# A four-layer transformer kernel on one core: table writes, recurrence steps and the order around two layer boundaries rearranged

## The chip, the core and the metric

The kernel runs on one core of a Trainium2 chip. The metric is the device time of one launch in microseconds. Each run is one execution; the figure shown is the median of three.

## What is computed

The reference takes 2048 tokens of 512 channels (8 sequences of 256) and sends them through four layers. Each layer has an attention-like part and a feed-forward part, both gated by a tanh and added to the tokens:

```python
x = x + tanh(g_xattn[0]) * L0_xattn(layernorm(x), ctx, ...)   # quantised attention
x = x + tanh(g_ffn[0])   * L0_ffn(layernorm(x), ...)          # one of 8 low-rank experts
x = x + tanh(g_xattn[1]) * L1_xattn(layernorm(x), ctx, ...)   # linear attention
x = x + tanh(g_ffn[1])   * L1_ffn(layernorm(x), ...)          # 8 of 64 experts, and a shared one
x = x + tanh(g_xattn[2]) * L2_xattn(layernorm(x), ctx)        # channels attend to channels
x = x + tanh(g_ffn[2])   * L2_ffn(layernorm(x), ...)          # dense, 2048 hidden units, GELU
x = x + tanh(g_xattn[3]) * L3_xattn(..., layernorm(x), ctx)   # a recurrence over 256 steps
x = x + tanh(g_ffn[3])   * L3_ffn(layernorm(x), ...)          # 2 of 8 experts, and a shared one
```

## The kernel before

**Tiles and blocks.** The tokens stay in SBUF as 16 tiles `xt[0..15]` of 128 tokens by 512 channels. Most loops run over 4 blocks of 512 tokens (`NB`, each `TB` = 4 tiles), and many over the 2 sequences of a block (`bb`). Matrix products go to PSUM banks of pools `mm` (4 banks), `ac` (2) and `tr` (2, for transposes).

**What sets the order.** The program is written as generators that interleave pieces of several stages, and a scheduler then orders the instructions of each engine: among those whose inputs it believes ready it takes the one that comes first in the program. Each engine then works strictly in its order, so an instruction that waits holds up all behind it. `behind(one, other, ...)` (line 131) forces `one` to stand after `other` in that order without a semaphore. `latest[0]` is the last matmul of the latest product.

**Layer 1.** `attend1` (833) does the attention of a block and calls `step`, which advances a generator of routing pieces and then, through `write` (945), issues rows of the routing table. A row write is an indirect DMA on POOL of 128 rows; it waits for the end of the product `latest[0]`. `route1(q)` (969) handles a pair of tiles q: norm, logits, the choice of 8 experts, the rows and weights (`hit`, line 1064), and it appends 16 writes to `pending`. The last pair, q = 7, writes its rows at once and also ranks the experts. `shared1(blk)` (1087) is the shared expert of a block in 5 pieces: gate, up, the remainder (which ends with the units `hT`, line 1110), and two down products of two tiles each, whose results are added by `add_scaled` (219) on DVE. After block 3's attention, the pieces of blocks 0 to 2 are interleaved with pair 7's routing and with `write(3, latest[0])` (1163). Then the table is read back (1177, `rows`, after all writes), turned by PE into `who_ps` (1193) and copied into `who` and `share`; each pair of experts gathers its tokens `xg` by `who` (1213). The experts' results are added in DRAM to two accumulators.

**The seam to layer 2.** After the experts comes `shared1` of block 3 (1336). `combine` (1344) loads the two accumulators (`more`) and adds them to the tokens on DVE. The first two tiles' combine is issued before the down products of block 3. Layer 2 then begins with `norm_of` for each sequence of block 0 (1729) and the scores.

**Layers 2 and 3 interleaved.** `xattn2` (1369) computes for each sequence of a block 4 score products (`s`), their maximum on DVE (1385), an exponential on ACT (1387, `E`), a scaling `vs` on DVE (1391), then 4 output products `o`. `ffn2` (1436) has 4 quarters of 4 hidden products `h2p` and 4 output products `o2f`. Meanwhile `step(n, one)` advances `tail(blk)`, which is layer 3 for the block before: the recurrence `xattn3` (1471), four channel groups with scans on DVE, products on POOL and an exponential on ACT, then turned by PE (`y`, 1543) and added; and the routing `route` (1621), which ends with 8 table writes on POOL (1669). `held` ties the first recurrence operation of a step behind `one`. At the last quarter's first output `last` flushes what is left with `step(1000)`. `ready2` (1416) norms a block for `ffn2` during the second half of `xattn2`. In block 3 the tail is interleaved with the shared expert `shared3`.

Of the kernel before, what the change touches and what calls it, by code (L numbers as in the profile page):

```python
# [20 lines left out]
P = 128  # L21
# [25 lines left out]
def flamingo_kernel(ctx: ExitStack, tc: tile.TileContext, a):  # L47
# [103 lines left out]
    def stats_of(ts_, name, after=()):  # L151
# [15 lines left out]
        yield ts_, mv, rstd  # L167

    def normed(stats, name, after=()):
        ts_, mv, rstd = stats  # L170
        out = []
        for i, t in enumerate(ts_):
            xn = xnp.tile([P, C], F32, tag="xn", name=f"xn_{name}_{i}")
            one = nc.vector.tensor_scalar(xn, xt[t], mv[:, i, 0:1], rstd[:, i : i + 1], ALU.subtract, ALU.mult)
            for other in after:
                behind(one, other, "the scores first")
            out.append(xn)
        return out

# [466 lines left out]
    def middle():  # L646
        with ExitStack() as st:
# [185 lines left out]
            def attend1(blk, one_step):  # L833
# [24 lines left out]
                for bb in range(BLK // S):  # L858
                    nm = f"{blk}_{bb}"
                    kf, V = context1(blk, bb, K, step) if bb else first  # L860
                    if blk == NB - 1 and bb:
                        step = lambda n: one_step(n, True)
# [65 lines left out]
                    for nt in range(2):  # L928
                        aoT = t2.tile([P, KC, P], F32, tag="t2", name=f"aoT_{nm}_{nt}")
                        aoTs.append(aoT)  # L930
                        transpose4(aoT, aos[nt].rearrange("p h d -> p (h d)"), f"ao_{nm}_{nt}")
                        step(1)
                    for nt in range(2):
                        ps = mmtile(f"wo1_{nm}_{nt}")
                        matmul_k(ps, [aoTs[nt][:, k, :] for k in range(KC)], [wo[:, k, :] for k in range(KC)])
                        i = blk * TB + bb * 2 + nt
                        add_scaled(i, ps, tg[:, 1:2])
                        step(2 if nt == 0 else 0)
                    done.append(blk * (BLK // S) + bb)
# [29 lines left out]
            def route1(q):  # L969
# [92 lines left out]
                for i in range(2):  # L1062
                    for j in range(K1):
                        nc.vector.scalar_tensor_tensor(
                            hit, key[:, i, :], key8[:, i, j : j + 1], w[:, i, :], ALU.is_equal, ALU.mult,
                            accum_out=pay[:, i, j, 1:2],
                        )
                    nc.vector.tensor_scalar(
                        pay[:, i, :, 1], pay[:, i, :, 1], den[:, i : i + 1], None, ALU.mult
# [9 lines left out]
                if q == 2 * NB - 1:  # L1079
                    ordered(expert)  # L1080
                    yield

            I1R = I1 - P
            rows_of = (slice(0, I1R), slice(FD, FD + I1R))
            rest1 = rows_of[1]

            def shared1(blk, shgu):

# [19 lines left out]
                for n in range(2):  # L1108
# [3 lines left out]
                    )  # L1112
                last_add[:] = [one]
                yield
                for i in range(0, TB, 2):
                    ps = [mmtile(f"shd{blk}_{i + n}") for n in range(2)]
                    last = None
                    for k in range(2):
                        for n in range(2):
                            rows = rows_of[n] if k else slice(0, P)  # L1120
                            one = nc.tensor.matmul(
                                ps[n], hT[k][rows, ts(i + n, P)], shd[rows, k, :], start=(k == 0), stop=(k == 1)
                            )
# [17 lines left out]

            last_add = []
            gen = work()
# [48 lines left out]
            for n in range(2):  # L1192
                one = nc.tensor.transpose(who_ps[:, n, :], rows[:, :, n], ident)
# [163 lines left out]

    kxvs, kx_load, first_loads = {}, [], []

# [9 lines left out]
    def xattn2(blk, xns, pools, step, ready=iter(())):  # L1369
# [4 lines left out]
        for bb in range(BLK // S):  # L1374
# [6 lines left out]
            for ec in range(KC):  # L1381
# [53 lines left out]

    def ffn2(blk, b8, wp, b1, gb2, step, last):
        xT = turned2.pop(blk)

        for q in range(HID // BLK):
            h = b8.tile([P, KC, BLK], F32, tag="b8", name=f"h2_{q}_{blk}")  # L1440
            p2 = []
            for j in range(KC):
# [109 lines left out]
    def back():  # L1552
        with ExitStack() as st:
# [63 lines left out]
            row_i = lp.tile([P, TT, 2], I32, tag="row3", name="row3")  # L1617
            writes = []
            xT = []

            def route(blk):
# [45 lines left out]
                for t in range(blk * TB, blk * TB + TB):  # L1667
                    for j in range(2):
                        one = nc.gpsimd.indirect_dma_start(
                            out=table[:, :],  # L1670
                            out_offset=bass.IndirectOffsetOnAxis(ap=row_i[:, t, j : j + 1], axis=0),
                            in_=pay[:, t, j, :],
                            in_offset=None,
                        )
                        tc.declare_no_dep(one.ins, group="table3", reason="choices have slots of their own")
                        tc.add_to_no_dep_group("table3", one.ins)
                        writes.append(one)
                    if t % 2:
                        yield

# [59 lines left out]
            for blk in range(NB):  # L1740
                ffn2(blk, fp, wp, b1, gb2, step, lambda i: last(blk + 2, i))
                rest.append(tail(blk))
# [83 lines left out]
            def shared3():  # L1826
# [5 lines left out]
                for blk in range(NB):  # L1832
                    xb = [xT[blk][:, k, :] for k in range(KC)]
                    hT = late.tile([P, 6, BLK], F32, tag="shT3", name=f"shT3_{blk}")
                    for m in (5, *range(5)):
# [13 lines left out]
                        else:  # L1849
# [248 lines left out]
```

## Time and profile before

| | us |
|---|---|
| median of 3 runs | 2705.74 (2701.91 to 2705.78) |
| the profiled execution | 2704.81 |
| its span, first to last instruction | 2703.0 |
| TensorE (PE) busy | 2553.9, 94% |
| VectorE (DVE) busy | 1288.3, 48% |
| GpSimd (POOL) busy | 890.6, 33% |
| ScalarE (ACT) busy | 671.9, 25% |
| mean granted TensorE clock | 0.974 |

Stages by time from the span's start: layer 0 to about 560, layer 1's attention to 911, shared expert and table to 984, layer 1's experts to 1491, the seam to 1518, layer 2 with the recurrence to 2145, layer 3's experts to the end.

In the profile, a group of instructions is named by its line, engine, operation and tiles. PEld is PE's weight load, SPq the queue of DMAs issued by SP. An idle time in brackets is the time that the engine stood before the instruction, and after the arrow what ended it. The granted clock is the share of full speed that TensorE was given.

### The profile page before, as it was taken

The page shows a single profiled execution, that of the slowest core. Times are in us where ns is not written, and L with a number is a line of the kernel's source. Part 1 is how long each engine was busy: PE and PEld are TensorE (multiplying, and loading weights), DVE is VectorE, ACT ScalarE, POOL GpSimd, SP SyncE. Part 2 cuts the span into 40 slices and gives each one's busy share as a digit, 9 for nine tenths or more (in the row PEclk, how much of TensorE's full clock was granted, in tenths as well). Part 3 has the DMA queues.
Part 4 walks back from the last instruction along what each step waited for, and adds up shares of the span by engine and source line. Part 5 has one row for each costly group of instructions (what it writes and reads, how often), then busy time and mean ns, then how long its engine had stood idle before and what let it go on. Part 6 is the DMA issues. An engine that isn't in the chain of part 4 may idle for free. (4 is left out here: it accounts for less than half of the span.)

```text
span 2703.0 us, 29475 instructions
## 1 busy us (share of the span) xinstructions
PE 2553.9 (94%) x10253; PEld 1355.1 (50%) x10268; DVE 1288.3 (48%) x3535; ACT 671.9 (25%) x1505; POOL 890.6 (33%) x814
## 2 busy tenths in 40 slices
PE   7889898999999899999999899898999999999998
PEld 3445444455665445555555344344454444455554
DVE  7656575536655622222222641767666674121121
ACT  2534344311111113333333211222223231111110
POOL 1111110112444445656565110333333342333332
PEclk9999899999999899999999999999999999999999
DMA  5000000112200259999997721132121211888884
GB/s 214 9 16 24 20 36 4 33 36 63 64 25 25 59 175 237 246 242 246 243 241 169 224 113 64 38 110 61 61 91 67 106 16 47 278 276 270 288 278 113
DMA packets 96187, 333.04 MB, mean 123 GB/s; under 512 B 20608, under 2 KB 23041, under 8 KB 88098
## 3 DMA queue, kind: packets, MB, share of 16 engines
q0 software_dynamic: 45856, 156.51, 23.0%
q1 hardware_dynamic: 47154, 170.34, 18.6%
q10 hardware_dynamic: 3024, 4.25, 0.5%
q8 instruction: 84, 1.38, 0.2%
q14 instruction: 69, 0.57, 0.1%
HBM read 280.46 MB, written 64.91 MB: 128 GB/s over the span
## 5 line engine op out<-in xcount | busy, mean ns | idle before, releaser
L210 PE MATMUL gu<-w,eb 128*128 128x352 f32 x896 | 285.9, 462 | 0.0
L1293 POOL DMA_INDIRECT acc<-eb,who x112 | 177.5, 1585 | 175.5 <-DVE eb L102 148.3
L210 PE MATMUL h2p<-xnT_f,p 128*128 128x512 f32 x512 | 228.0, 601 | 3.0 <-ACT xnT_f L104 3.0
L210 PE MATMUL o2f<-p,h 128*128 128x512 f32 x512 | 224.8, 593 | 0.0
L210 PEld LDWEIGHTS gu<-w,eb 128*128 128x128 f32 x896 | 162.6, 192 | 73.4 <-issue 2.3
L950 POOL DMA_INDIRECT table<-pay,rowi x128 | 126.1, 985 | 120.6 <-issue 26.1
L539 ACT ACTIVATE pr<-pr,n 128x256 f32<-128x256 f32 x256 | 127.9, 501 | 151.7 <-DVE n L534 148.8
L210 PEld LDWEIGHTS h2p<-xnT_f,p 128*128 128x128 f32 x512 | 97.2, 192 | 120.8 <-issue 115.7
L210 PEld LDWEIGHTS o2f<-p,h 128*128 128x128 f32 x512 | 96.2, 190 | 117.4 <-issue 115.2
L1213 POOL DMA_INDIRECT xg<-xnd,who x112 | 117.2, 1046 | 59.6 <-PE ehp L1240 22.8
L221 DVE SCALAR_TENSOR_TENSOR x<-o2f,tg,x 128x512 f32<-128x512 f32 x64 | 47.0, 739 | 140.7 <-PE o2f L210 140.7
L1768 PE MATMUL g_r<-w,xgT 128*128 128x352 f32 x288 | 111.7, 469 | 0.7 <-ACT xgT L104 0.7
L1768 PE MATMUL u_r<-w,xgT 128*128 128x352 f32 x288 | 108.7, 459 | 0.0
L1284 PE MATMUL ed<-w,eb 128*128 128x512 f32 x224 | 105.7, 594 | 0.9 <-DVE eb L1241 0.9
L102 DVE COPY eb<-ed 128x512 f32<-128x512 f32 x56 | 38.7, 692 | 138.6 <-PE ed L1284 138.6
L1775 DVE SCALAR_TENSOR_TENSOR h_r<-a_r,share,u_r 128x352 f32<-128x352 f32 x36 | 20.9, 581 | 175.9 <-PE u_r L1768 167.4
L1791 PE MATMUL d_r<-w,hT_r 128*128 128x512 f32 (+1 forms) x216 | 104.2, 592 | 0.0
L534 DVE CUSTOM_DVE_ANT_0 pr<-s,mask 128x256 f32<-128x256 f32 x256 | 96.9, 417 | 12.2 <-PE s L514 8.8
L1230 DVE SCALAR_TENSOR_TENSOR eb<-eb,share,gu 128x176 f32<-128x176 f32 x112 | 44.0, 393 | 122.0 <-ACT eb L1229 122.0
L591 POOL TENSOR_TENSOR y<-y,gbo 128x512 f32<-128x512 f32 x16 | 20.4, 1272 | 246.8 <-DVE y L590 239.0
L188 PEld LDWEIGHTS tr_xg<-ident,xg 128*128 128x128 f32 x592 | 68.9, 141 | 63.2 <-issue 49.9
L188 PE MATMUL tr_xg<-ident,xg 128*128 128x128 f32 x592 | 92.7, 280 | 6.4 <-DMA xg<-xnd,who 6.3
(534 smaller groups left out, 4730.5 us busy)
## 6 DMA issues: line engine op xcount, KB each, us to landing
w<-in_w SPq DMA_DIRECT2D x64, 960.0 KB, 7.3
p<-in_p SPq DMA_DIRECT2D x64, 512.0 KB, 5.7
xnd<-xn_f SPq DMA_DIRECT2D x32, 256.0 KB, 3.2
acc<-xnd SPq DMA_DIRECT2D x32, 256.0 KB, 4.9
more<-acc SPq DMA_DIRECT2D x32, 256.0 KB, 4.3
wd<-in_wd SPq DMA_DIRECT2D x64, 96.0 KB, 6.9
ctxTa<-in_ctxT SPq DMA_DIRECT2D x4, 1024.0 KB, 6.0
x<-in_x SPq DMA_DIRECT2D x16, 256.0 KB, 5.9
```

Source lines behind the costliest of these rows:

```text
L188: one = nc.tensor.transpose(ps[:, k, :], src[:, ts(k, P)], ident)
L210: one = nc.tensor.matmul(ps, lhsT[k], rhs[k], start=(k == 0), stop=(k == n - 1))
L221: return nc.vector.scalar_tensor_tensor(xt[i], ps, scale, xt[i], ALU.mult, ALU.add)
L534: one = nc.vector.tensor_tensor_reduce(pr[:, nt, :], ps[r][:, nt, :], mask[:, nt, :], -1.0, -LOW, ALU.add, ALU.min, n16[:, nt, h : h + 1],)
L539: nc.scalar.activation(pr[:, nt, :], pr[:, nt, :], AF.Exp, bias=n16[:, nt, h : h + 1], scale=-1.0, accum_out=s16[:, nt, h : h + 1],)
L950: one = nc.gpsimd.indirect_dma_start(out=table[:, :], out_offset=bass.IndirectOffsetOnAxis(ap=rows, axis=0), in_=choice, in_offset=None, b ...
L1213: nc.gpsimd.indirect_dma_start(out=xg, out_offset=None, in_=xnd[:, :], in_offset=bass.IndirectOffsetOnAxis(ap=who[:, c : c + 1], axis=0), ...
L1230: nc.vector.scalar_tensor_tensor(self.h, self.h, share[:, c : c + 1], gu[:, I1 : 2 * I1], ALU.mult, ALU.mult)
L1284: one = nc.tensor.matmul(ps[n], t.hT[rows, k, :], wd, start=(k == 0), stop=(k == 1))
L1293: nc.gpsimd.indirect_dma_start(out=acc[n][:, :], out_offset=bass.IndirectOffsetOnAxis(ap=who[:, t.c : t.c + 1], axis=0), in_=t.x, in_offse ...
L1768: nc.tensor.matmul(ps[:, 0:I3], xTt[:, k, :], wgu[k][:, g, :], start=(k == 0), stop=(k == KC - 1))
L1791: one = nc.tensor.matmul(ps, hT[:cn, n, :], wd[n][:cn], start=(n == 0), stop=(n == 2))
```

## The change

- `attend1`: in the second sequence of block 3 (`quiet`), the steps at the turned outputs and at the output product issue no table writes; they still advance the routing.
- `route1`: pair 7's first hit is ordered behind the shared expert's units made last (`hidden`).
- The table is read and turned before the two down products of block 2: only 13 of the 15 pieces of `shared1` run first, and the first of the remaining matmuls stands behind the turned order. `who` stands behind the units and no longer behind the adds.
- `shared1` of block 3 uses the `ac` banks for its first two tiles and leaves its four adds in a list; they are issued in layer 2 behind the last normed tile of the first two tiles (`latest_norm`).
- `combine` adds the tiles of blocks 2 and 3 on POOL instead of DVE.
- `xattn2`: no step during the second sequence's scores.
- `route`: the 8 table writes of a block go to a list. `ffn2` and, for block 2's, `shared3` issue one after each hidden (or gate and up) product of the next block, each waiting for that product's end. The last block's are issued at once.

```diff
-                    if blk == NB - 1 and bb:
+                    quiet = blk == NB - 1 and bb
+                    if quiet:
                         step = lambda n: one_step(n, True)
...
-                        step(1)
+                        step(0 if quiet else 1)
...
-                        step(2 if nt == 0 else 0)
+                        step(0 if nt or quiet else 2)
...
+                        if hidden and i + j == 0:
+                            behind(one, hidden[0], "the shared expert's first")
...
-            def shared1(blk, shgu):
+            def shared1(blk, shgu, later=None):
...
-                last_add[:] = [one]
+                hidden[:] = [one]
                 yield
                 for i in range(0, TB, 2):
-                    ps = [mmtile(f"shd{blk}_{i + n}") for n in range(2)]
+                    bank, tag = (mm, "mm") if i or later is None else (ac, "ac")
+                    ps = [bank.tile([P, BLK], F32, tag=tag, name=f"shd{blk}_{i + n}") for n in range(2)]
...
+                            if turned:
+                                behind(one, turned.pop(), "the table's order first")
...
-                        one = add_scaled(blk * TB + i + n, ps[n], tg[:, 5:6])
-                        if i + n == 0:
-                            behind(one, last_add[0], "its place")
-                        last_add[:] = [one]
+                        if later is None:
+                            add_scaled(blk * TB + i + n, ps[n], tg[:, 5:6])
+                        else:
+                            later.append((blk * TB + i + n, ps[n], tg[:, 5:6]))
...
-            while next(two, 0) is None:
+            for _ in range(5 * (NB - 1) - 2):
+                next(two)
                 write(3, latest[0])
                 with tc.high_priority(offset=400):
                     next(one, 0)
...
+            turned.append(one)
             who = l2.tile([P, P], I32, tag="who", name="who")
             one = nc.vector.tensor_copy(who, who_ps[:, 0, :])
-            behind(one, last_add[0], "the table comes late")
+            behind(one, hidden[0], "the table comes late")
             share = l2.tile([P, P], F32, tag="share", name="share")
             nc.scalar.copy(share, who_ps[:, 1, :])
+            for _ in two:
+                pass
...
-            end = shared1(NB - 1, again)
+            end = shared1(NB - 1, again, last_adds)
             for _ in range(3):
                 next(end)
-            first_loads.append(combine(range(2), adds=last_add))
+            first_loads.append(combine(range(2), adds=hidden))
...
-                add = nc.vector.tensor_tensor(xt[t], xt[t], more, ALU.add)
+                add = (nc.vector if t < 2 * TB else nc.gpsimd).tensor_tensor(out=xt[t], in0=xt[t], in1=more, op=ALU.add)
...
                 if bb:
                     latest_dve[:] = [one]
                     next(ready, None)
-                step(1, one)
+                else:
+                    step(1, one)
...
                 step(2 if q < 1 else 3, one)
+                write(1, latest[0])
...
+                    pending3.extend((row_i[:, t, j : j + 1], pay[:, t, j, :]) for j in range(2))
+                if blk == NB - 1:
+                    write3(len(pending3))
+                yield
+
+            def write3(n, after=None):
+                for _ in range(min(n, len(pending3))):
+                    rows, choice = pending3.pop(0)
+                    one = nc.gpsimd.indirect_dma_start(
...
+                    if after is not None:
+                        tc.add_manual_dep(
...
                 xns += norm_of(tiles, f"a2{bb}_")
+                other = latest_norm[0]
+                for add in last_adds:
+                    behind(add_scaled(*add), other, "layer 2's first tokens first")
+                last_adds.clear()
...
                         last_mul[:] = [one]
+                        write3(1, latest[0])
                         yield
```

More of the change, by code (lines that the diff above doesn't have):

```diff
@@ L167, in stats_of @@
         yield ts_, mv, rstd
+    latest_norm = []
     def normed(stats, name, after=()):
@@ L177, in normed @@
             out.append(xn)
+        latest_norm[:] = [one]
         return out
@@ L1063, in route1 @@
                     for j in range(K1):
-                        nc.vector.scalar_tensor_tensor(
+                        one = nc.vector.scalar_tensor_tensor(
                             hit, key[:, i, :], key8[:, i, j : j + 1], w[:, i, :], ALU.is_equal, ALU.mult,
@@ L1081, in route1 @@
                     yield
+            turned = []
+            hidden = []
             I1R = I1 - P
@@ L1140, in work @@
                     yield from route1(q)
-            last_add = []
             gen = work()
@@ L1356, in combine @@
         return one
-    kxvs, kx_load, first_loads = {}, [], []
+    kxvs, kx_load, first_loads, last_adds = {}, [], [], []
     def load_kx(b, b8, after=None):
@@ L1434, in ready2, with ffn2 @@
                 yield
-    def ffn2(blk, b8, wp, b1, gb2, step, last):
+    def ffn2(blk, b8, wp, b1, gb2, step, last, write):
         xT = turned2.pop(blk)
@@ L1617, in back @@
             row_i = lp.tile([P, TT, 2], I32, tag="row3", name="row3")
-            writes = []
+            writes, pending3 = [], []
             xT = []
@@ L1667, in route @@
                 for t in range(blk * TB, blk * TB + TB):
[L1668 to L1673, printed above, removed]
-                        )
[L1675 to L1679, printed above, removed]
+                    pending3.extend((row_i[:, t, j : j + 1], pay[:, t, j, :]) for j in range(2))
[6 more added lines that the diff above has]
+                    one = nc.gpsimd.indirect_dma_start(
+                        out=table[:, :],
+                        out_offset=bass.IndirectOffsetOnAxis(ap=rows, axis=0),
+                        in_=choice,
+                        in_offset=None,
+                    )
+                    if after is not None:
+                        tc.add_manual_dep(
+                            one.ins,
+                            after.ins.name,
+                            mybir.DependencyInfo(mybir.DependencyClass.Sync, mybir.DependencyReason.DATA),
+                            reason="one after the other",
+                        )
+                    tc.declare_no_dep(one.ins, group="table3", reason="choices have slots of their own")
+                    tc.add_to_no_dep_group("table3", one.ins)
+                    writes.append(one)
             def tail(blk):
@@ L1740, in back @@
             for blk in range(NB):
-                ffn2(blk, fp, wp, b1, gb2, step, lambda i: last(blk + 2, i))
+                ffn2(blk, fp, wp, b1, gb2, step, lambda i: last(blk + 2, i), write3)
                 rest.append(tail(blk))
```

## The prediction

> **What bounds the kernel now.** I read the page's busy table, then the waits of PE, then busy time and clock by stage, then the order of instructions around each long wait of PE.
>
> ```profile
> PE 2553.9 (94%) x10253; PEld 1355.1 (50%) x10268; DVE 1288.3 (48%) x3535; ACT 671.9 (25%) x1505; POOL 890.6 (33%) x814
> ```
>
> TensorE works 2553.9 of 2703.0 us. A time saved elsewhere counts only if PE waits for it; the chain of waits on the page names only the last store, so I go by PE's waits (what waits on what: total, times, longest).
>
> ```profile
> PE s L210 <- DMA kxvs<-in_ctx: 8.0, 2, 6.1
> PE tr_f L188 <- DVE xn_f L174: 8.0, 5, 5.3
> ...
> PE tr_xg L188 <- DMA xg<-xnd,who: 6.3, 1, 6.3
> PE o L210 <- ACT E L1387: 6.0, 2, 5.7
> ...
> PE shd L1121 <- DVE shT L1110: 3.4, 1, 3.4
> ```
>
> Five single waits of 3.4 to 6.1 us, and one of 5.25 us at 1517.71, lie where the diff works. Each costs more than itself. By stages (start:end, length, busy of PE, PEld, DVE, ACT, POOL, granted clock, DMA share, GB/s):
>
> ```profile
> 936.00:948.00 12.00, 11.91 (x19) 4.18 (x20) 5.63 (x24) 0.00 (x0) 7.26 (x8) 0.60 0.02 3
> ```
>
> A granted 0.60 over 12 us means 9.6 us at half speed, right after the 3.40 us wait at 936.09; the same follows the waits at 916.96, 983.86, 1517.71 and 1713.00. Half of such a stretch is lost work. Now the order of events (start, length, engine, what, idle before and its releaser):
>
> ```profile
> 914.49 0.97 POOL L950 DMA_INDIRECT table<-pay,rowi  x1 [0.30 <-issue]
> 915.48 0.75 POOL L166 TENSOR_TENSOR rstd_f<-ve_f,mhalf 128x2 f32<-128x2 f32 x1
> ...
> 916.96 1.94 PE L188 MATMUL tr_f<-ident,xn_f 128*128 128x128 f32 x8 [5.32 <-DVE xn_f L174]
> ...
> 964.76 1.02 POOL L1177 DMA_INDIRECT rows<-table,row_c  x1 [6.03 <-DMA table<-pay,rowi]
> ...
> 977.01 0.51 PE L1193 MATMUL who_ps<-ident,rows 128*128 128x128 f32 x2
> ```
>
> ```profile
> 1710.61 0.69 DVE L1511 TENSOR_TENSOR_SCAN aa<-ex,ev 128x256 f32<-128x256 f32 x1 [2.58 <-POOL ev L1508]
> 1711.22 0.67 DVE L1385 TENSOR_REDUCE m<-s 128x1 f32<-128x512 f32 x1
> ...
> 1713.00 12.56 PE L210 MATMUL o<-E,kxvs 128*128 128x512 f32 x24 [5.66 <-ACT E L1387]
> ```
>
> See in the first: the norm's power waits in POOL's queue behind table writes, PE behind it; and the table's rows were asked for at 964.76 but turned only at 977.01. In the second: a maximum of the second scores, which PE had ready near 1702, stands on DVE behind a recurrence scan.
>
> **Part 1, the quiet last block.** Eight writes (905.51 to 914.49, 1.275 us apart) leave POOL's queue there. The variances are ready at 911.0, so the power starts near 911.2 instead of 915.48 and PE goes on at 912.6: 4.3 us. The slow stretch 917 to 922 (transposes 1.94 against 1.04, shg 1.92 against 1.02, logits 2.54 against 1.89) goes: 2.45. The eight writes come back later on the same queue, see Part 3.
>
> **Part 2, the hits after the shared expert's units.** Units shT were made at 935.62, behind 8 hits and the ranking; their input was ready at 930.5. Put first, they leave PE about 0.6 of the 3.40: 2.8 us. From 936.09 to the next product at 947.94 PE took 11.85 us for ten down matmuls (10/16 of 5.84) and eight of 3.44 in all, 7.1 us: 4.75 more. The hits start 0.9 us later (two multiplications); nobody but the table's writes needs them. Parts 1 and 2: 14.3 us, so PE ends block 2's last shared product at 971.17 - 14.3 = 956.9.
>
> **Part 3, the table's order before the last two down products.** Now 32 writes (16 of tile pair 6, 16 of pair 7) follow one another on POOL from 914.8: 32 x 1.275 = 40.8, plus some 2 of waits for products, the last at 956 instead of 957.75. The weight loads that ran beside the old last writes (landing 5.9) start with `order`, now some 14 us sooner, so I take the usual 2.1 to land and 2.8 for the read (its row): rows at 961. PE waits there about 4.1 (new: before, the rows had 9.4 us to spare). Behind the order come 5.84 us of products, slowed by up to 2.9, beside the 6.34 us of copy, gather and landing that PE waited for bare. Gather transposes then start at 961 + 1.0 + 8.2 = 970.2 at full clock; before, 983.86 and 6.4 us at half speed, worth 987.1. **Saved 16.9 us** for Parts 1 to 3. Bounds: 23.3 if the rows are in time (956.9 + 0.5 + 6.34 = 963.7); 7.6 if writes and landing are late by 9 (979.5). I take 16.9, by the rows' usual landings. The experts' stage after it runs PE at 200.00 of 200.00 us, so it only shifts.
>
> **Part 4, the seam.** Four of block 3's adds (0.75 + 2.06 us on DVE) leave the way of the first norm: scores start at 1514.6 instead of 1517.71. But the second pair's norm has the same DVE work in front, now with those adds: ready near 1524.4, where PE came at 1527.04 (slow). Two of the four product banks are held until the adds; DVE gets there before the third score. So PE saves some 2.5 (0 to 5.6, the latter with the slow stretch gone too).
>
> The clock page speaks against this part. The Trainium skill, "TensorE: Matmul & The Clock Gate", section "HAM oscillation", lets the clock fall after idle gaps above some 3.4 us; the new gap of about 3.0 would then cost nothing more, and the part would be worth 5. The rows say less: 2.34 and 2.58 us of waiting at 169 and 174 were followed by half speed.
>
> **Part 5, sixteen combine adds from DVE to POOL.** DVE's takes 0.684; POOL's two-operand form 1.26 alone to 1.71 beside DVE: 20 to 27 us on an engine busy 12.64 of 100 us in 1500 to 1600. On SP the `more` loads wait for buffers that those adds free; kxvs, ctxT and p loads stand behind. The last `more` went at 1550.9 and PE then waited 1.98 for kxvs; with POOL adding from about 1531 it goes no later. Value: 1.5 saved (2.0 to minus 5, if a norm's power queues behind several adds).
>
> The Trainium skill, "GPSIMD Engine Reference", section "Engine selection", keeps two-input elementwise work on VectorE, GPSIMD being about twice as slow. The trace agrees on the size (1.27 to 0.684); followed, it would forbid the move, and the sum would lose this part's 1.5.
>
> **Part 6, steps off the second scores.** Four steps fewer per block, so steps 5 to 8 lie on the outputs and all later ones four calls later; 8 + 57 = 65 steps are there before the flush, and the tail has 65. What held the maximum of 1711.22 back were scans (0.68 each) and the 2.58 us wait of a scan that nothing ties to its step: the scheduler took it when its inputs were ready, whatever its step. The first of a step's held operations alone is tied. I therefore keep the 5.66 us wait and its slow 2.1 (12.56 against 10.46). What does go are the held scans and num (1.09 + 1.64) that kept the copy of 1731.55 back: PE's 2.40 at 1732.27, and 2.08 at 1895.90: **4.5 us**. Bounds: 0, and 19.9 if the scores' waits for E go too: 5.66 + 2.1, and in the later block 7.65 more (outputs at 1871.2 instead of 1879.05, less Part 7's 0.2).
>
> **Part 7, layer 3's writes.** At 1845 to 1855 eight writes ran beside kxvs' load: it took 15.4 us, against 6.9 one block earlier without them. With the writes gone PE's 6.07 goes, but the same maximum then rules as at 1713.00: outputs at 1864.1 + 12.7 = 1876.8 instead of 1879.05, less 2.1 of slow clock. **0.2 us.** The new wait: each write waits for its product's end (3.44 us apart); behind it on POOL queue the recurrence's ex, ev, den and products, and behind those DVE's scans and PE's turned channels. Hidden while the recurrence keeps its pace; bare otherwise (the slower rival). The writes in shared3 wait likewise; the table's read comes over 100 us later. Longer life of row_i and pay costs no buffer.
>
> **Sum:** 16.9 + 2.5 + 1.5 + 4.5 + 0.2 = 25.6 us off the profiled execution's 2704.81 (span 2703.0 and 1.8 around it): 2679.2. The median shown is 0.93 above that execution: 2680.
>
> **Rivals.**
> - *The second scores run free* (Part 6's upper end). For it: the four steps are what stood there in the code. Against: 1710.61's scan ran before its own step's turn. 2680 - 15.4 = 2665.
> - *The table rules layer 1's end*: 32 rows queue behind products, the last ones late, PE idles ahead of the order. For it: POOL stood 4.67 and 2.23 us for products at 920.90 and 926.71; against: rows are only some 4 us short already. 2680 + 9.3 = 2689.
> - *Slower: late recurrence.* In layer 3 a channel takes 20 us at the end of a block (1787.29 to 1808.95) with DVE, ACT and POOL in one chain, so it can't catch up; its last result (1808.95 + 1.27) leads PE's turn of it (1811.45) by 1.2 us, and by 1.2, 1.1 and 2.1 in the other blocks. If four steps' delay and the POOL waits make it L late beyond what its steps moved, each of four tails stalls PE L - 1.2 and costs 3.4 of slow clock, as after 2143.08. It cancels the rest at L = 4.2 and makes the kernel measurably slower from 5.6; at L = 8 it costs 40.8: 2720.
> - *It does not do what it says:* the scheduler's new order gives back elsewhere what layer 1 gains: 2704.
>
> **How the numbers follow.** Forecast 2680: 0.45 (own range 2672 to 2689). Free scores 2665: 0.22. Table 2689: 0.16. Cancelled 2704: 0.05. Late recurrence 2720: 0.12. Measurement tells 0.2%, 5.4 us, from no change: faster 0.83, same 0.05, slower 0.12. The range takes the first three with their bounds: 2657 (free scores with Part 3's upper end in part) to 2698, leaving out 0.17.
>
> **What would show it.** After: rstd within a microsecond of its variance near 911; no wait for shT; PE waiting for the table's rows about 4 us, then none over 1 for xg; gather transposes near 970; the first layer 2 scores 3 us nearer to the shared products; kxvs landing in 7 us and the wait for it replaced by one for E of some 5.6 in both blocks; no wait of 2 us for xnT_f. I am wrong if PE waits for y's channels in layer 3, if the rows come after 966, or if the E waits vanish.

## The result, and the profile after

The changed kernel takes 2689.11 us (median of 5 runs, 2687.79 to 2691.45); beside it the kernel before took 2702.36 (2700.86 to 2705.78). The ratio is 0.9946, with a 95% interval of 0.9935 to 0.9957: faster by 13.25 us. The profiled execution took 2687.79 with a span of 2686.1, so between the two profiled executions the difference is 17.0: the one of before was 2.45 above its median, the one of the changed kernel 1.32 below its own. Ratios, here and below, are not quotients of the two medians and can differ a little from them.

PE works about as long as before; what went is waiting and slow clock. From the page of the changed kernel:

```profile
PE 2546.7 (95%) x10253; PEld 1350.5 (50%) x10268; DVE 1283.3 (48%) x3519; ACT 668.5 (25%) x1503; POOL 913.7 (34%) x830
```

Its waits of PE (what waits on what: total, times, longest):

```profile
PE o L213 <- ACT E L1401: 11.1, 2, 5.7
...
PE s L213 <- DMA kxvs<-in_ctx: 3.6, 1, 3.6
...
PE tr_xg L191 <- DMA xg<-xnd,who: 3.3, 2, 2.3
PE o2f L213 <- ACT h L1467: 3.2, 3, 1.2
...
PE who_ps L1204 <- DMA rows<-table,row_c: 2.6, 1, 2.6
```

Gone are the two waits for the copies of xnT_f (2.40 and 2.08). The wait for shT is 0.77 instead of 3.40, that for xn_f 0.90 instead of 5.32, that for xg 2.32 and 0.95 instead of 6.34. The waits for E are now two of 5.65 and 5.48. New are those for the table's rows and, three times, for h.

Where the 16.9 us of the spans lie shows best by landmarks of PE, counted from one to the next:

| stretch, from one landmark to the next | before | after | difference |
|---|---|---|---|
| start to the shared expert of block 3 (shg) | 1494.48 | 1482.82 | -11.66 |
| to the first hidden product of layer 2 (h2p), the seam | 86.06 | 86.87 | +0.81 |
| to layer 3's first shared product (sg), the recurrence and writes | 564.64 | 561.43 | -3.21 |
| to the end | 557.82 | 554.98 | -2.84 |

These are single executions. Of the first 11.66 us, 0.95 lie in code that the change does not touch: PE stops for the last norm of layer 1 at 911.64 before and at 910.69 after, and 0.91 of this lead is there at 563 us already. In a second trace of the changed kernel (e5, below) the last three stretches are 87.35, 563.67 and 556.03, so they vary by 0.5 to 2.2 us with the same code. PE's idle time in the third is steadier: 26.3 before, 23.2 and 23.4 in the two traces after.

The end of layer 1 in the changed kernel, in order of events (start, length, engine, what, idle before and its releaser):

```profile
910.14 0.72 POOL L166 TENSOR_TENSOR rstd_f<-ve_f,mhalf 128x2 f32<-128x2 f32 x1 [7.85 <-DVE ve_f L164]
```

```profile
911.59 1.08 PE L191 MATMUL tr_f<-ident,xn_f 128*128 128x128 f32 x8 [0.90 <-DVE xn_f L176]
...
925.78 6.52 PE L1130 MATMUL shd<-shd,shT 48*128 48x512 f32 x10 [0.77 <-DVE shT L1118]
...
962.78 0.51 PE L1204 MATMUL who_ps<-ident,rows 128*128 128x128 f32 x2 [2.56 <-DMA rows<-table,row_c]
...
971.36 0.66 PE L191 MATMUL tr_xg<-ident,xg 128*128 128x128 f32 x4 [2.32 <-DMA xg<-xnd,who]
972.97 1.09 PE L191 MATMUL tr_xg<-ident,xg 128*128 128x128 f32 x4 [0.95 <-DMA xg<-xnd,who]
```

The norm's power follows its variance at once, PE hardly waits for shT, and the down products stand between the rows and the gathers, as the change means them to. But the down matmuls of 925.78 take 6.52 us for ten, hardly less than the 7.20 that the same ten took before, where sixteen take 5.91 at 963.13. By stages (start:end, length, busy of PE, PEld, DVE, ACT, POOL, granted clock, DMA share, GB/s):

```profile
928.00:935.00 7.00, 7.00 (x11) 2.37 (x11) 5.07 (x25) 0.00 (x0) 4.86 (x5) 0.54 0.02 2
...
972.00:979.00 7.00, 6.05 (x17) 3.96 (x17) 0.69 (x1) 0.80 (x2) 2.00 (x2) 0.52 1.01 372
```

Half speed is left in two stretches, the first after a wait of only 0.77 us. The second stretch shows a full DMA system (share 1.01): eight weight loads were issued from 962.76 on, and the first gathers, issued among them, took 8.3 us (median of four) to land, against 3.6 in the kernel before, where the last of the loads had been issued 2.9 us ahead of the first gather.

### The profile page after: what moved, and what is told of

Read it like the earlier page. It is cut to its first block, busy times and chain, and to the rows that moved or that the text cites. A ratio compares the mean times of both kernels' runs of the same rounds, so it can differ in the third digit from the quotient of the medians.

```text
span 2686.1 us, 29479 instructions
## 1 busy us (share of the span) xinstructions
PE 2546.7 (95%) x10253; PEld 1350.5 (50%) x10268; DVE 1283.3 (48%) x3519; ACT 668.5 (25%) x1503; POOL 913.7 (34%) x830
## 3 DMA queue, kind: packets, MB, share of 16 engines
q0 software_dynamic: 45856, 156.51, 23.4%
## 5 line engine op out<-in xcount | busy, mean ns | idle before, releaser
L954 POOL DMA_INDIRECT table<-pay,rowi x128 | 126.0, 984 | 113.0 <-issue 23.6
L191 PEld LDWEIGHTS tr_xg<-ident,xg 128*128 128x128 f32 x592 | 68.9, 141 | 61.0 <-issue 51.2
L166 POOL TENSOR_TENSOR rstd_a<-ve_a,mhalf 128x4 f32<-128x4 f32 x15 | 15.3, 1021 | 243.7 <-DVE ve_a L164 243.6
```

The lines of the kernel that those rows point to most:

```text
L191: one = nc.tensor.transpose(ps[:, k, :], src[:, ts(k, P)], ident)
L954: one = nc.gpsimd.indirect_dma_start(out=table[:, :], out_offset=bass.IndirectOffsetOnAxis(ap=rows, axis=0), in_=choice, in_offset=None, b ...
```

## The experiments

They ran on three chips, four on each, with the kernel before beside them: on the chip of the first four it takes 2728.56 us, on that of the next four 2703.99, on that of the last four 2729.40. The changed kernel itself was run again on the second alone.

**The change's own gain on another chip.** e5_after_again, no edit.

> The changed kernel, unaltered, beside the other runs of this call; the first four ran on a chip where the kernel before takes 2728.6 us instead of 2702, so the change's own gain has to be seen on the chip where its parts are undone. Theory (the gain is the changed order's own): the ratio to before is 0.9946 again, within 0.001. Rival (the gain hangs on how the instruction fetch and the loads happen to fall at layer 1's end): a ratio of 0.998 or more on a chip that is slower.

Measured: 2689.47 (2687.02 to 2696.28), ratio 0.9951 (0.9939 to 0.9964). The gain is that of the first measurement, 14.5 us here by the medians. That this chip is no slower one left the rival untried.

**Parts 1 to 3 undone together**, twice, on the two slower chips: e1_layer1_back and e9_layer1_back2.

```diff
-                        step(0 if quiet else 1)
+                        step(1)
...
-                        step(0 if nt or quiet else 2)
+                        step(2 if nt == 0 else 0)
...
-                        if hidden and i + j == 0:
-                            behind(one, hidden[0], "the shared expert's first")
...
-                            if turned:
-                                behind(one, turned.pop(), "the table's order first")
...
-            for _ in range(5 * (NB - 1) - 2):
-                next(two)
+            while next(two, 0) is None:
```

> Undoes Parts 1 to 3 alone (writes paced as before in the last block, hits where they were, the table's order behind all of block 2's products); all else is the changed kernel. Theory (layer 1's end brought some 11 of the 17 us that lie between the two profiled executions, the rest came later): 2689 + 11 = 2700, gather transposes again near 984, all later landmarks about 11 us later. Rival (most of it came from the recurrence and the seam): no more than 2694. Rival (the forecast's own 16.9 was there and a later loss ate 5): 2706.

> Parts 1 to 3 undone together, once more beside later runs, because on the slower chip all differences were within 0.1%. Theory (the recurrence's parts are worth 6.4 us and the seam's nothing, so layer 1's end is worth the rest of the 13 to 14.5, some 8): a ratio to before near 0.9976, 8 us over the changed kernel. Rival (traces: the gather transposes' 11 to 12 us): 0.9988. Rival (the forecast's 16.9): slower than before.

Measured: ratios 0.9997 (0.9985 to 1.0009) and 0.9980 (0.9970 to 0.9989). With layer 1's end undone the rest is worth some 1 and 5 us of 2729 there (3 and 4 by the medians), two measurements whose intervals hardly meet. Against the changed kernel nothing can be said by time, since it did not run on those chips. The traces give a length that does compare: from where PE stops for the last norm to the first gather's transposes.

| kernel | chip | us |
|---|---|---|
| before | that of the first measurement | 72.2 |
| changed | that of the first measurement | 60.7 |
| changed (e5), and with layer 1 unaltered e6, e7, e8 | second | 60.5, 60.6, 60.8, 60.6 |
| Parts 1 to 3 undone (e1, e9) | slower | 70.9, 70.8 |
| Part 3 undone (e2, e10) | slower | 68.9, 69.0 |
| layer 1 as changed (e3, e4) | slower | 69.7, 68.0 |
| as changed, with the loads moved (e11, e12) | slower | 62.0, 69.7 |

Where before takes 2702 to 2704 the three parts are worth 11.4 to 11.8 us of this stretch in five traces, set against one of before. These three parts were not undone there, so that the gain is their own is read from the rows and not tested by time; what the two experiments of Parts 4 to 7 (below) leave of e5's 14.5 us for them is 8.7, an estimate that takes the parts to add up, and uncertain by some 5. On the slower chips the same order is worth 1 to 3. What stands there instead shows in the run with the loads moved (below), on one of those chips:

```profile
984.43 0.75 DVE L224 SCALAR_TENSOR_TENSOR x<-shd,tg,x 128x512 f32<-128x512 f32 x1 [7.96 <-remote]
```

```profile
985.24 5.31 PE L213 MATMUL shg<-xnT_f,rwsh 128*128 128x512 f32 x8 [2.97 <-DVE x L224]
```

DVE stood 7.96 us before an add whose product, by the lengths of its matmuls, PE had done near 978; what released it the profile only calls remote, and PE waited for the bank that this add frees. All six traces of the slower chips with the quiet block and the hits in place have such waits of DVE here (2.8 to 11.4 us); the two with Parts 1 to 3 undone, and the traces of the other chips, have none. Its cause was not found.

**Part 3 alone undone**, also twice on those chips: e2_order_last and e10_order_last2. The edit is the last two hunks above.

> Undoes Part 3 alone: the table's order again behind the last two down products, with the quiet norm and the hits behind shT kept. Theory (the 5.9 us of products cover most of the copy, the gather and its landing; the gain of the order is real, less what the new waits of 2.56, 2.32 and 0.95 us and their slow clock take): rows turned near 966 instead of 962.8, first gather landing near 973 to 975, so 2 to 5 us slower, 2691 to 2694. Rival (the order in front brought nothing, since PE now waits for the rows and still for the gather): within 1 us of 2689.

> Part 3 alone undone, once more beside the run with all three undone. Theory: the order in front is worth 2 to 5 us, a ratio of 0.9956 to 0.9968, and the quiet norm with the hits the rest. Rival (Part 3 brought nothing; its new waits ate it): 0.995.

Measured: 0.9995 (0.9983 to 1.0006) and 0.9983 (0.9970 to 0.9997), in both cases within 0.0003, under 1 us, of the ratio with all three undone. What the quiet norm and the hits bring on those chips without Part 3 is too small to show (the intervals leave 3 to 4 us either way; the stretch above is 2 us shorter); what Part 3 is worth there stays open, for the same reason as above.

**The loads beside the gathers.** e11_loads_behind_xg:

```diff
-                    nc.gpsimd.indirect_dma_start(
+                    one = nc.gpsimd.indirect_dma_start(
                         out=xg,
...
+                    if c == 1:
+                        table_read[:] = [one]
```

> One added edit to the changed kernel: the expert weights that waited for the table's read wait for the second tile's gather. Theory (eight weight loads, 4.2 MB issued from 962.76 on, delay the first gathers, 7.4 us to landing against 4.9 in the kernel before): gathers land in 5 us, PE's waits of 2.3 and 1.0 to 1.5 for xg shrink below 1 in all and the half clock behind them goes, 3 to 6 us under the changed kernel, a ratio of 0.993 to 0.994. Rival (the loads, begun 5 us later, are late for the third and fourth pairs, which PE then waits for): no gain, 0.995 or more.

Measured: 0.9954 (0.9939 to 0.9970), which has no changed kernel beside it. The trace decides. PE's transposes of the first two gathers, and the granted clock of the stretch behind them:

```profile
1004.06 0.66 PE L191 MATMUL tr_xg<-ident,xg 128*128 128x128 f32 x4
1005.22 0.63 PE L191 MATMUL tr_xg<-ident,xg 128*128 128x128 f32 x4 [0.51 <-issue]
```

```profile
1003.00:1010.00 7.00, 6.12 (x28) 3.72 (x28) 2.77 (x5) 1.52 (x3) 4.37 (x5) 1.00 0.80 247
```

No wait for xg is left and the clock is 1.00 where it was 0.52. From the rows' turn to the first transposes it is 6.07 us, the length of the down products alone, against 8.58 in the changed kernel; by the third gather's transposes 5.1 us are saved. No wait of PE over 0.8 us follows in the experts' stage, so the loads are not late there. The chip does not explain it: on the slower ones the distance from the rows' turn to the first transposes is 8.5 and 10.4 with the loads where they were (e3, e4) and 6.1 in both traces with the loads moved (this one and e12). So the loads held the gathers back, and by these traces they cost the changed kernel 5.1 us here; a time beside the changed kernel is lacking.

**The seam.** e3_dve_adds (Part 5 undone, slower chip) and e6_seam_back (Parts 4 and 5 undone):

```diff
-                add = (nc.vector if t < 2 * TB else nc.gpsimd).tensor_tensor(out=xt[t], in0=xt[t], in1=more, op=ALU.add)
+                add = nc.vector.tensor_tensor(out=xt[t], in0=xt[t], in1=more, op=ALU.add)
```

and, in e6_seam_back, besides it:

```diff
-            end = shared1(NB - 1, again, last_adds)
+            end = shared1(NB - 1, again)
```

> Undoes Part 5 alone: all combine adds on DVE. Theory (the POOL adds hold buffers of the loads longer and slow DVE beside them, and gave the seam's 3 us back): the wait for kxvs of 3.6 us shrinks to 2 or less, normalizations near 1535 take 1.9 us again instead of 5.7, and the time is 2 to 4 us less, 2685 to 2687. Rival (the forecast's: POOL adds save 1.5): 2690 to 2691.

> Undoes Parts 4 and 5: block 3's adds in their place, all combine adds on DVE; all else changed. Theory (the seam's 3 us were given back through the loads behind POOL's adds): within 1 us of the changed kernel in the same call; the first scores of layer 2 start 3 us later after the shared products, kxvs is waited for 2 us or less, and the first products after the second block's attention stand as after the change. Rival (the forecast: the two parts save 2.5 + 1.5): 4 us slower than the changed kernel.

Measured: e3 0.9968 (0.9956 to 0.9980), e6 0.9949 (0.9935 to 0.9962), which is 2688.93 beside 2689.47 for the changed kernel. By time the two parts together are worth nothing that shows, but with six runs of each, whose ranges span 9 and 11 us, the forecast's 4.0 is not excluded either. The traces say more. Their stretch, counted from shg of block 3:

| kernel | first scores | first h2p |
|---|---|---|
| before | 23.2 | 86.06 |
| changed (in brackets all 10 traces with both parts) | 20.4 (18.7 to 20.4) | 86.87 (86.87 to 88.62) |
| Part 5 undone (e3; e12, with two other edits) | 20.1; 21.6 | 85.45; 85.21 |
| Parts 4 and 5 undone (e6) | 23.8 | 85.85 |

Part 4 brings its 3 us at the first scores, with the adds on either engine (1.6 in e12, whose first products run at half speed for 6.8 us and not 3.4). A third is lost at once: the four adds that it moved, 2.73 us, stand on DVE ahead of the first maximum, and PE waits 1.44 us for the first E before it goes on with the second sequence's scores (1.43 to 1.52 in all twelve traces with Part 4, none in before and e6). The rest is gone by h2p where POOL adds. DVE and POOL in the changed kernel, then DVE with the adds back on it (e6):

```profile
1530.85 5.71 DVE L176 TENSOR_SCALAR xn_a<-x,mv_a,rstd_a 128x512 f32<-128x512 f32 x4 [1.14 <-POOL rstd_a L166]
```

```profile
1530.79 14.59 POOL L1366 TENSOR_TENSOR x<-x,more 128x512 f32<-128x512 f32 x11
```

```profile
1537.05 1.45 DVE L176 TENSOR_SCALAR xn_a<-x,mv_a,rstd_a 128x512 f32<-128x512 f32 x3
```

Four normalizations take 5.71 us beside the adds, 1.43 each; three take 1.45 without them. POOL's adds are 1.33 apart, so each normalization lasts about as long as one add. The Trainium skill, "SBUF — State Buffer", section "Who interferes with whom", says that VectorE in some modes, `tensor_scalar` among the operations named, shares a pair of ports with GpSimd, held by one of them for a whole instruction; these rows agree. The `more` loads then hold SP up to 1538.0, and kxvs goes at 1538.60 and is waited for:

```profile
1544.73 8.80 PE L213 MATMUL s<-xn_a,kxvs 128*128 128x512 f32 x16 [3.58 <-DMA kxvs<-in_ctx]
```

The same wait is 1.07 in e6, 2.13 in e3 (its theory had 2 or less) and 2.10 in e12, and 3.6 to 4.1 wherever POOL adds; in e3 three normalizations take 1.46 again. Its time has no changed kernel beside it. By this table Part 5 costs 1.4 us or more, and without it Part 4 still has 0.6 to 0.9 of its gain at h2p; since the ten traces with both parts spread over 1.75, the second figure is not shown.

**Parts 6 and 7 undone.** e7_l3_back:

```diff
-                else:
-                    step(1, one)
+                step(1, one)
...
-                if blk == NB - 1:
-                    write3(len(pending3))
-                yield
+                    if t % 2:
+                        write3(len(pending3))
+                        yield
```

> Undoes Parts 6 and 7: steps on both rows of scores, and each block's eight writes in a row. Theory (what went are the waits of 2.40 and 2.08 us for turned units; the wait for kxvs only changed place with that for E, so the writes are worth nothing by themselves): 3 to 5 us slower than the changed kernel in the same call, with a wait of 6 us for kxvs in block 3 again, its landing 15 us. Rival (slow clock after it and the later waits of about 1 us for h take the gain back): within 2 us. Rival (the writes were worth more, because kxvs also held the stage behind it): 7 us or more.

Measured: 2695.85 (2692.04 to 2700.51), ratio 0.9978 (0.9969 to 0.9987) beside 0.9951: 6.4 us by the medians, above the theory's 3 to 5 but, with the scatter of the runs, not apart from it. As it said, kxvs lands 17.2 us after its issue (6.8 in the changed kernel); the landing in e7, then in the changed kernel (KB, us to landing):

```profile
kxvs<-in_ctx SPq DMA_DIRECT2D x1, 512.0 KB, 17.2
```

```profile
kxvs<-in_ctx SPq DMA_DIRECT2D x1, 512.0 KB, 6.8
```

And PE waits for it:

```profile
1861.12 10.03 PE L213 MATMUL s<-xn_a,kxvs 128*128 128x512 f32 x16 [7.94 <-DMA kxvs<-in_ctx]
```

The wait for E in block 3 is then gone, and waits for turned units (1.33 and 1.22) are back; the waits for h are not there. These came with the later steps. ACT in the changed kernel, ahead of PE's 1.21 at 1930.05:

```profile
1924.64 1.28 ACT L1521 ACT_TABLE_LOAD   x1 [2.80 <-DVE ex L1515]
1926.09 1.91 ACT L1521 ACTIVATE ex<-ex 128x2048 f32<-128x2048 f32 x1 [0.17 <-POOL ex L1517]
1928.02 1.28 ACT L1467 ACT_TABLE_LOAD   x1
1929.31 0.69 ACT L1467 ACTIVATE h<-h2p,b 128x512 f32<-128x512 f32 x1
```

The recurrence's exponential stands between two GELUs with a table load on each side, 4.7 us in all, and PE waits 1.21 us for the last h behind it.

**What holds E.** e4_held_all ties all held operations of a step; e8_aa_ex_tied ties both aa scans and the first channel's exponential:

```diff
-                        place.pop().ins.name,
+                        place[0].ins.name,
```

```diff
-                held(nc.vector.tensor_tensor_scan(
+                spot(nc.vector.tensor_tensor_scan(
                     out=aa[:, b, 1:],
...
-            nc.scalar.activation(ex, ex, AF.Exp)
+            one = nc.scalar.activation(ex, ex, AF.Exp)
+            if c == 0:
+                held(one)
```

(`spot` is `held` with the step's place even if another operation has used it.)

> One added edit to the changed kernel: each held operation of a recurrence step is tied to the step's place, not the first alone, so that no scan is hoisted ahead of the second scores' maximum. Theory (the waits of 5.65 and 5.48 us for E stand because an untied scan of aa, waiting for ev, is in front of the maximum on DVE): the maximum comes near 1696.5, E follows ACT's long exponential at 1698.4, the wait is 2.5 to 3 us in both blocks, and with less slow clock the time is 6 to 9 us less, 2680 to 2683. Rival (ACT's exponentials or the freed bank rule, not the maximum): waits of 5 us stay and the time within 1 us. Rival (the scans tied to later places make the recurrence late): waits for turned channels near 1830 and 2110, 2692 or more.

> Two added edits to the changed kernel: both scans of aa are tied to their step's place, not the first sequence's alone, and the first channel's long exponential is tied as well. Tying all scans cut both waits for E (to 2.46 and 1.75 us) but made the channels late, with waits of 2.5 and 2.9 us for h instead of 0.9 and 1.2. Theory (the aa scan is what held the maximum back, and ACT's exponential of 1.91 us is next): both waits for E 1.5 us or less, waits for h no longer than 1.5, and the time 6 to 10 us under the changed kernel's in the same call. Rival (the recurrence, begun 3 us later, is late again in both blocks): waits for h of 2.5 us or more and a gain under 3 us.

Measured: e4 0.9992 (0.9983 to 1.0001) on the slower chip; both waits for E fell to 2.46 and 1.75, and waits for h rose to 2.54 and 2.85. From h2p to sg it took 563.75 us, against 560.8 to 562.1 in five of the six other runs on slow chips that keep Parts 6 and 7 without ties, and 567.1 in the sixth. The theory was right on the waits; its 6 to 9 us can't be set against the changed kernel there, and the stretch says that the gain was given back. e8: 2684.44 (2683.02 to 2686.60), ratio 0.9935 (0.9923 to 0.9947), 5.0 us under the changed kernel beside it (the theory had 6 to 10), with no run of either in the other's range. The scores' maximum and the outputs, in the changed kernel (DVE, then PE) and in e8 (DVE, ACT, PE):

```profile
1699.76 0.69 DVE L1527 TENSOR_TENSOR_SCAN aa<-ex,ev 128x256 f32<-128x256 f32 x1 [2.58 <-POOL ev L1524]
1700.36 0.67 DVE L1399 TENSOR_REDUCE m<-s 128x1 f32<-128x512 f32 x1
```

```profile
1702.14 4.22 PE L213 MATMUL o<-E,kxvs 128*128 128x512 f32 x5 [5.65 <-ACT E L1401]
```

```profile
1698.46 0.67 DVE L1399 TENSOR_REDUCE m<-s 128x1 f32<-128x512 f32 x1
```

```profile
1699.41 0.69 ACT L1401 ACTIVATE E<-s,m 128x512 f32<-128x512 f32 x1 [5.69 <-DVE m L1400]
```

```profile
1700.24 1.98 PE L213 MATMUL o<-E,kxvs 128*128 128x512 f32 x4 [2.37 <-ACT E L1401]
```

With the scan away the maximum comes right behind the recurrence's earlier operations, and the wait is 2.37 (2.18 in the later block). The theory's 1.5 was too low: those operations, up to 1698.5, still stand before the maximum. The waits for h are 2.5 and 1.7, more than it allowed, and take part of the gain.

**All three edits.** e12_all_three joins the ties, the adds on DVE and the loads behind the gathers.

> The changed kernel with the aa scans and the first long exponential tied, all combine adds on DVE, and the expert weights behind the second gather. If the gains add: 5.0 from the ties, 3 to 6 from the loads, 0 to 2 from the adds, so 8 to 13 us under the changed kernel, 2676 to 2681 where before takes 2703, a ratio of 0.990 to 0.992. If the loads and adds bring nothing: 0.9935 as with the ties alone.

Measured: 0.9938 (0.9921 to 0.9955) on the slower chip, some 4 us under e11, hardly more than the scatter of the two. The hoped-for 0.990 to 0.992 was not reached: in its trace DVE waits 11.44 us for a remote release and PE 5.04 at layer 1's end. Of the versions run, e8 is the one shown to beat both kernels on one chip.

## Why the prediction was right, and where its sizes were off

The direction and range were right; the forecast of 25.6 us was nearly twice the 13.25 measured, and 2689 lies at the far edge of the forecast's own range of 2672 to 2689. Step by step:

**Parts 1 to 3, 16.9 forecast, 10.7 in the trace** (11.66 less the 0.95 from ahead of the changed code). The mechanism was right: power at 910.14, transposes at 911.59, shT's wait 0.77, last write 956.88, rows turned at 962.78 where 961 was worked out. Part 1's two terms, 4.3 and 2.45, came as 4.4 and 2.3, and Part 2's 2.8 as 2.6. Two steps failed. The first is Part 2's "4.75 more": the slow stretch behind the wait for shT was counted as gone with the wait, but it stands at 928 to 935 behind 0.77 us, and from the ten down matmuls to the next product PE took 11.06 us instead of 7.1 (11.85 before). So PE ended the shared products at 960.2, not 956.9; since the rows ruled there, this alone cost little. The step that cost was Part 3's "gather transposes then start at [...] full clock". They start 8.58 us behind the rows' turn, where the sum allowed 9.2; but the gathers land beside eight weight loads which the earlier table read sets free, so PE waits a second time (0.95), and the clock is 0.52 over 972 to 979, 3.4 us lost of a 6.8 us stretch. The rows themselves came 2.7 us late (with the lead of 0.95 counted), 1.8 of it at the last write. That is about the shortfall of 6.2. e11 takes the loads away, and its trace is 5.1 us shorter there.

**Part 4, 2.5 forecast.** At the first scores it is 2.9, as worked out; at the second ones 1.9, because the moved adds delay the first maximum on DVE, which the sum left out. By h2p nothing is left, and no more than 0.9 with the adds on DVE.

**Part 5, 1.5 gained forecast, 1.4 or more lost.** That kxvs "goes no later" held by the clock: from shg of block 3 it goes at 55.8 us, and at 56.8 before. What failed is to count the wait for it as saved: Part 4 had brought PE there 2.5 us earlier and kxvs went only 1.0 earlier, so PE waits 3.58 for it where it waited 1.98, and the scores behind it take 8.80 us instead of 7.10. With the adds on DVE it goes 1.3 us sooner (54.5 in e3). The slowing of DVE beside POOL was left out of the sum. Both parts together were put at 4.0 and were 0.5 the other way in e6, which does not exclude either.

**Part 6, 4.5, and Part 7, 0.2.** The waits of 2.40 and 2.08 went, and the wait for E stayed in both blocks (5.65, 5.48), behind the scan that was named. kxvs lands in 6.8 (7 forecast), and its wait of 6.07 became one for E. Not foreseen were the three waits for h, 3.2 us together. Together the two parts measured 6.4 in e7 against 4.7. In the traces the stretch to sg gives 3.2, but e5 and e7 have 563.7 and 563.6 there, and two other traces that keep both parts (e2, e6) have 567: half speed falls differently from one execution to the next. What holds is PE's idle time, 26.3 and 26.6 us in before and e7 against 23.2 to 23.6 in all nine traces that keep Parts 6 and 7 without ties: 3 us. The 2.8 us after sg are covered by a stretch of half speed near 2274 in before, in which PE loses 3.4:

```profile
2273.00:2281.00 8.00, 8.00 (x23) 4.88 (x23) 2.74 (x10) 1.95 (x3) 0.00 (x0) 0.57 0.03 5
```

e7 has it too (128 us after sg in both), and none of the twelve traces that keep Parts 6 and 7 has it. So it goes with these parts; PE's order there is the same in both kernels, and why the clock falls in one and not in the other is not shown.

**Rivals.** The table ruled layer 1's end by 2.56 us of waiting, less than that rival's case, yet its time of 2689 is what was measured, for other reasons: that is luck. Late recurrence did not come: no wait for y's channels. The scores did not run free. Of the signs promised, "then none over 1 for xg" failed (2.32), the rows were waited for 2.56 us and not about 4, and the scores' 3 us came but did not last. One reading of the lines was off: the five single waits run up to 6.3 us (for xg), not 6.1.

What stays open: what the remote waits of DVE are, and so how much the change gives on the slower chips, where it was not run unaltered; and Parts 1 to 3, the largest share, by time on a chip where the change pays.

## What to carry to other kernels

When a step is moved earlier, list what its completion sets free: here the table's earlier read released eight loads onto the very gathers that the move was to speed up. A gain at one landmark is to be followed to the next place where PE waits, since 3 us at the first scores had vanished 67 us later behind a load that went only 1 us earlier. And an operation that nothing ties to its place will be put wherever its inputs seem ready, so look at the order on the engine for what stands ahead of the one that matters.

## What the runs showed of the hardware

- Half speed came without a long wait: after 0.77 us idle the clock was 0.54 over 928 to 935, behind the stretch from 922 in which four short products of 0.19 to 0.22 us stand. In before it came without any: PE stood idle for no more than 0.15 us at a time from 2196 to 2281, and the clock was 0.57 from 2273 on, behind transposes and products of 8 columns. The Trainium skill, "TensorE: Matmul & The Clock Gate", section "HAM oscillation", speaks of idle gaps above some 3.4 us; these rows show it with less, and with none.
- The same program is 25 us slower on two of the chips. In their traces most of it is lost from 690 to 900 us, at the last five of layer 1's eight groups of 64 small kf products. In e4 each of these five takes 3.6 to 4.5 us instead of 1.94, with stops of 0.3 us in it that the profile puts down to issue, and the products behind run at half speed; together 21 us. One such place (the changed kernel's row first; the lines have the same six products):

```profile
740.68 2.84 PE L213 MATMUL v<-Wv,ctxTb 128*128 128x512 f32 x6
```

```profile
745.65 4.29 PE L213 MATMUL v<-Wv,ctxTb 128*128 128x512 f32 x6 [0.29 <-issue]
```

- One load of 512 KB, four others issued just ahead of it, took 17.2 us to land (15.4 in before) beside eight indirect table writes, the last of which landed 12 us after the load's issue, and 6.8 with the same four loads and no writes.
